# Value weights loaded as the second key stage opens, layer 0 four products later, the second attention step's exponentials among its products, one rotation put off

## The chip, the cores and the metric

The kernel runs on one core of a Trainium2 chip. A core has five engines with a queue of instructions each: TensorE (PE, matrix products into PSUM banks), VectorE (DVE), ScalarE (ACT), GpSimd (POOL) and SyncE (SP), which here only issues DMAs. ACT and POOL issue DMAs too. Each queue runs in its own order, and engines wait for one another by semaphores. The metric is the time of one execution on the device in microseconds.

## The reference

Two sequences of 512 rows of 1024 (`x`) and two contexts of 1024 rows of 1024 (`ctx`) run through four blocks, each added to `x`:

```python
x = x + fake_quant(layernorm(x)) @ fake_quant(ctx)                 # layer 0, part 1
x = x + layernorm(x) @ W.T + b + lora(layernorm(x)) * routing      # layer 0, part 2
q = rope(layernorm(x) @ wq)      # 32 heads of 128
k = rope(ctx @ wk)               # 8 key heads, each used by 4 query heads
v = ctx @ wv                     # 8 value heads
x = x + (softmax(q @ k.T / sqrt(128) + mask) @ v) @ wo
x = x + layernorm(x) @ W_up.T + lora of the top expert
```

Keys and values depend on the context only, so they can be computed before layer 0 has ended.

## The kernel before

**Products.** The large products of keys, values, queries, both linear maps and the output projection are done with seven products in place of eight (Strassen-Winograd). Sums of quarters of each operand are made first, on DVE (`left_steps`, `right_steps`), and `seven` or `seven_onto` then runs one generator per block of the output: each `yield` is one product, which the trace shows as 8 matmuls of 128x512 for keys and queries (4 in the code, an f32 one has two records) and 16 of 128x256 for values, into one of four PSUM banks of the tag "b". The results are put together by adds on DVE and a copy on ACT (lines 284 to 300), which also give the banks back. The other four PSUM banks are two double banks of the tag "wide", used for transposes and for attention's scores.

**Order of work.** PE's order is written out by hand: it is the order in which the program emits its instructions. The other engines are ordered by a scheduler, in two stretches excepted: the first key stages, and attention, where DVE and ACT (in attention POOL as well) run in emission order too.

**Stages.** Per sequence `b` there are two key stages and two value stages (`keys`, `keys`, `values`, `values`; `i` from 0 to 3), each with 14 products. `pair` interleaves the first two products of the two blocks of a stage. `weave(main, side, every)` runs a stage and calls `next(side)` after every second product. `side` is `layer_0()`: the quantized product of both sequences (`quantized_product`), cut by yields into small steps: loads of two context rows and their quantization on DVE (lines 194 to 198), layernorms of `x` (lines 163 to 176), transposes on PE (`turned`, line 423) with a copy and a row sum on ACT, then the products (line 460). The weights of a stage are loaded and summed by `quad_weights` after the stage before has been emitted: four DMAs of 512 KB on SP's queue (line 362) and four passes of DVE (lines 245 to 253, `quad_sums`). SP's queue also holds the writes of the keys to DRAM (line 486), the loads of context rows for layer 0 (line 413), and the writes of values.

**Rotations.** Keys and queries are rotated (`rope_steps`, lines 213 to 223): two copies on ACT swap the halves (216, 217), a pass of DVE multiplies by the cosine (219), and a multiply and an add on an engine of choice (222, 223) finish it. Queries are made for eight groups `q` of four heads (`queries`). For `q` below 7 all of a rotation is emitted at once on DVE. For `q` = 7 the products run inside attention, the second half of each rotation is put into a list `later`, and its multiply and add go to POOL; attention empties the list in the third phase of each step (`rotate`).

**Attention.** 64 heads run as a pipeline over steps `n` from -2. In step `n`, head `n+2` gets its scores (4 pairs of matmuls, line 759, and the add of the mask on DVE, 773), its maximum (`tree`, 781 to 787, then transposes 723 and a reduction 725), which travels to a row in DRAM and back to all partitions (`to_row`, line 732; `from_row`, line 738). Head `n+1` subtracts it (`place_maximum` copies it into a "b" bank, 801; `exponential`, 805 on DVE, 808 on ACT, sums on POOL 811 to 816). Head `n` multiplies by the values (822), turns its sum of exponentials into a reciprocal, sends it to a row (`turn_sum`) and reads it back (`old.den = from_row(old.den)`), and is normalized on POOL in the next step (833). Both reads and both row writes are on ACT's queue. A step has three phases, ended by yields: scores; tree, projection products (or, in the first steps, `extra` products of the last queries); and the third phase shown at lines 923 to 944.

The lines that the change touches in the stages are these:

```python
 weave(main, side, 2)
 if i < 3:
     w = quad_weights((wk, wv)[(i + 1) // 2], (i + 1) % 2)
```

and `extra = {-2: 3, -1: 3, 0: 2, 1: 2, 2: 2, 3: 1, 4: 1}`, the number of query products that each attention step takes in its second phase.

Of the kernel before, what the change touches and what calls it, by code (L numbers as in the profile page):

```python
# [21 lines left out]
NH, NKV, DH = 32, 8, 128  # L22
# [17 lines left out]
def decoder_kernel(  # L40
# [25 lines left out]
    nc = tc.nc  # L66
# [268 lines left out]
    def weave(main, side, every, skip=0):  # L335

        for i, _ in enumerate(main):
            if i >= skip and (i - skip) % every == 0:
                next(side, None)
# [15 lines left out]

    def quad_weights(dram, q):

        raw = []
        for mh in range(2):
            for ch in range(2):  # L360
                w = u4([P, 4, 256])
                nc.sync.dma_start(w, dram[q, mh, ch])
                raw.append(w)
        return quad_sums(raw)

    def quad_sums(raw):
        return left_sums(nc.vector, *raw, lambda: u4([P, 4, 256]))
# [288 lines left out]
        yield  # L656


    def queries(q, h_ops, w, later=None):

        def head(m):
            def product(i, acc, start):
                accumulate(
                    acc,
                    [(w[i - 1][:, c, ts(m, P)], h_ops[i - 1][:, c, :]) for c in range(4)],
                    start,
                )

            def finish(i, j, src):
                dst = u2([P, HALF]) if (i, j) == (0, 0) else src  # L670
                eng = nc.vector if later is None else nc.gpsimd
                yield from rope_steps(dst, src, 0, ATT_SCALE, eng)
                nc.sync.dma_start(q_d[j][4 * q + 2 * i + m], dst)

            def emit(i, j, src):
                steps = finish(i, j, src)
                next(steps)
                if later is None:
                    next(steps, None)
                else:  # L680
                    later.append(steps)

            return seven(product, emit)

        return head(0), head(1)
# [49 lines left out]
    def from_row(row):  # L735

        t = u2([P, S])
        nc.scalar.dma_start(t, row.partition_broadcast(P))
        return t
# [107 lines left out]
    def attention(extra):  # L847

        total = B * NH
        heads, outs, kv = {}, {}, {}
        stretches = iter(())

        def rotate():
            for rotation in extra["later"]:
                next(rotation, None)
            extra["later"].clear()

        def begin(n):
            if n >= total:
                return
            gg = n // GRP
            if gg not in kv:
                b, g = gg // NKV, gg % NKV
                kT = u4([P, S2])
                nc.sync.dma_start(kT, kT_d[b][g])
                v = u4([P, NKT, DH])
                nc.sync.dma_start(v, v_d[b][g // 2][:, :, ts(g % 2, DH)])  # L870
                kv[gg] = kT, v
                outs[gg] = u8([P, GRP, S])
            heads[n] = Head(n, kv[gg], outs[gg][:, n % GRP, :])

        begin(0)
        for n in range(-2, total + GRP + 1):
            new, mid, old = heads.get(n + 2), heads.get(n + 1), heads.get(n)
            begin(n + 3)
            if new:
                for j in range(4):  # L880
                    new.scores(j)
            yield

            if n - 1 in heads:
                heads.pop(n - 1).normalize()
            if n == GRP - 1 or n == NH:
                fetch_rows(n // NH)

            if GRP <= n <= total and n % GRP == 0:
                oT = outs.pop(n // GRP - 1)  # L890
                sums = u8([P, 3, 2, 256])
                places = iter(range(3))
                o_ops = left_sums(
                    nc.gpsimd,
                    oT[:, 0:2, 0:256],
                    oT[:, 2:4, 0:256],
                    oT[:, 0:2, 256:S],
                    oT[:, 2:4, 256:S],
                    lambda: sums[:, next(places)],
                )  # L900
                following = n // GRP - 1, o_ops
            tree = new.tree() if new else iter(())
            k = (n - 1) % GRP
            if n > GRP and k == 0:
                gg, o_ops = following
                stretches = projection(gg // NKV, o_ops, dict(w_ops))
            for _ in range(3 + k % 2 if n > GRP else 0):
                next(stretches, None)
                next(tree, None)
            if n > GRP and gg + 1 < B * NKV:  # L910
                for i in {2: (1, 6, 2), 3: (7, 5, 4, 3)}.get(k, ()):
                    w_ops[i] = output_operand((gg + 1) % NKV, i)
            for _ in range(extra.pop(n, 0)):
                for _ in range(2):
                    next(tree, None)
                next(extra["products"])
            if n == GRP:
                w_ops = {i: output_operand(0, i) for i in (1, 6, 2, 7, 5, 4, 3)}
            for _ in tree:
                pass  # L920
            yield

            if mid:
                mid.place_maximum()
            if old:
                old.turn_sum()
            elif new:
                new.turn_maximum()
            rotate()
            if old:  # L930
                old.attend(0)
            if mid:
                mid.exponential(0)
            if old:
                old.den = from_row(old.den)
                if new:
                    new.turn_maximum()
            if mid:
                mid.exponential(1)
            if new:  # L940
                new.nmx = from_row(new.nmx)
            if old:
                old.attend(1)
            yield
# [85 lines left out]
    w = [wk_raw[q][0:2] + [None] * 5 for q in range(2)]  # L1030
# [33 lines left out]
    side = layer_0()  # L1064
    for b in range(B):
        if b == 1:
            for ch in range(2):
                ctx_raw[2 * ch + 1] = context_quarter(1, ch, 1, nc.scalar)
            w = quad_weights(wk, 0)
            ctx_ops = context_sums(ctx_raw)  # L1070
        for i, stage in enumerate((keys, keys, values, values)):
            if (b, i) == (0, 0):
                continue
            if (b, i) == (0, 3):
                ctx_raw = [None] * 4
                for ch in range(2):
                    ctx_raw[2 * ch] = context_quarter(1, ch, 0, nc.scalar)
            if (b, i) == (0, 1):
                main = chain(*first[1])
            else:  # L1080
                main = pair(*stage(b, i % 2, ctx_ops, w))
            weave(main, side, 2)
            if i < 3:
                w = quad_weights((wk, wv)[(i + 1) // 2], (i + 1) % 2)
            if i == 1 and b == 1:
                for _ in side:
                    pass
                ab_t = u8([P, 2, D])
                a_t, b_t = ab_t[:, 0].rearrange("p (c m) -> p c m", c=NC), ab_t[:, 1]
                nc.sync.dma_start(a_t, a0T.rearrange("(c p) m -> p c m", p=P))  # L1090
                nc.gpsimd.dma_start(b_t, b0.partition_broadcast(P))
                tT = [None] * B
                fetch_rows(0)
                hs, steps = normed(0, u8, 2)
                side = chain(steps, routed(0, hs, a_t, b_t, tT))
# [18 lines left out]
    for b in range(B):  # L1114
        main = linear(b, token_sums(hs, eights()), w_ops, lambda: tT[b], bl_t)
# [10 lines left out]
    w = [quad_weights(wq, 0), quad_weights(wq, 1)]  # L1126
    side = query_norm(1)
    h_ops = [hb[0][0], hb[0][1]] + [None] * 5
    early = [head for q in range(2) for head in queries(q, h_ops, w[q])]
    for _ in range(2):  # L1130
        for head in early:
            next(head)
# [4 lines left out]
    )  # L1137
    later = []
    for q in range(NH // 4):
        heads = (  # L1140
            early[2 * q : 2 * q + 2]
            if q < 2
            else queries(q, h_ops, w, later if q == NH // 4 - 1 else None)
        )
        main = chain(*heads) if q < 2 else pair(*heads)
        for g in ((0,), (1,), (2,), (3,), (4,), (5,), (6, 7), ())[q]:
            output_sums(g)
        if q < NH // 4 - 1:
            for _ in main:
                pass  # L1150
            if q > 0:
                w = quad_weights(wq, q + 1)

    extra = {-2: 3, -1: 3, 0: 2, 1: 2, 2: 2, 3: 1, 4: 1}
    steps = attention({**extra, "products": main, "later": later})
    stats = all_moments(0)
    last = {"zT": [None] * B, "w": [None] * 7, "h": [None] * 7}
# [186 lines left out]
```

## Time and profile before

| | us |
|---|---|
| median of three runs | 2475.18 (2473.69 to 2479.97) |
| profiled execution | 2474.92 |
| its span | 2473.1 |
| PE busy in it | 2432.6 (98%) |
| DVE busy | 1835.2 (74%) |
| POOL busy | 1028.8 (42%) |
| ACT busy | 528.1 (21%) |
| granted clock of PE, mean | 0.993 |

The profile is of one execution. Its times start at the span's beginning. The stages of the first sequence's keys and values lie between 0 and some 225 us (the first value stage begins at 109), those of the second follow, the queries end at about 928 where attention begins, attention's last step ends near 2300, and the last linear map fills the rest. A busy share counts the time in which an engine works on an instruction; an idle stretch of PE stands in brackets ahead of the row that ended it, with the instruction whose end released it. Idle time of another engine costs nothing by itself; it matters only where PE waits for it.

### The profile page before, as it was taken

The page shows a single profiled execution, that of the slowest core. Times are in us where ns is not written, and L with a number is a line of the kernel's source. Part 1 is how long each engine was busy: PE and PEld are TensorE (multiplying, and loading weights), DVE is VectorE, ACT ScalarE, POOL GpSimd, SP SyncE. Part 2 cuts the span into 40 slices and gives each one's busy share as a digit, 9 for nine tenths or more (in the row PEclk, how much of TensorE's full clock was granted, in tenths as well). Part 3 has the DMA queues.
Part 4 walks back from the last instruction along what each step waited for, and adds up shares of the span by engine and source line. Part 5 has one row for each costly group of instructions (what it writes and reads, how often), then busy time and mean ns, then how long its engine had stood idle before and what let it go on. Part 6 is the DMA issues. An engine that isn't in the chain of part 4 may idle for free.

```text
span 2473.1 us, 19694 instructions
## 1 busy us (share of the span) xinstructions
PE 2432.6 (98%) x6856; PEld 1218.4 (49%) x6856; DVE 1835.2 (74%) x2020; ACT 528.1 (21%) x615; POOL 1028.8 (42%) x552
## 2 busy tenths in 40 slices
PE   8999999999999999999999999999999999999998
PEld 3477458654444444444444444444444444445453
DVE  4949674346886547898888888888888888886552
ACT  1211221001122222222222222222222222222100
POOL 0000010111000002686767767776767676767421
PEclk9999999999999999999999999999999999999999
DMA  5437142013895221344323432443334333323301
GB/s 181 179 120 255 69 146 97 22 68 111 296 333 187 74 98 41 106 128 115 103 76 90 115 95 81 128 149 89 105 110 129 79 94 108 112 72 103 128 26 43
DMA packets 148819, 288.02 MB, mean 116 GB/s; under 512 B 29360, under 2 KB 47296, under 8 KB 146416
## 3 DMA queue, kind: packets, MB, share of 16 engines
q1 hardware_dynamic: 107888, 244.35, 29.4%
q10 hardware_dynamic: 40400, 41.70, 6.9%
q8 instruction: 55, 0.90, 0.2%
q0 software_dynamic: 432, 0.71, 0.1%
q14 instruction: 44, 0.36, 0.1%
HBM read 223.54 MB, written 63.18 MB: 116 GB/s over the span
## 4 chain that ended last, share of the span: by engine, by line
PE 79%; DVE 8%; POOL 3%; issue 2%; DMA 2%; ACT 1%; SPq 0%; ACTq 0%; POOLq 0%; DVEq 0%
PE b L347 45%; PE wide L759 15%; PE b L822 14%; DVE u L805 2%; PE wide L723 2%; PE wide L460 1%; PE wide L204 1%; POOL u L815 1%; POOL u L814 1%; DVE u L783 1%; DMA u<-in_wo_dram 1%; DVE u L785 1%; PE wide L954 1%; DVE small L725 1%; DMA row<-small 1%
## 5 line engine op out<-in xcount | busy, mean ns | idle before, releaser
L347 PE MATMUL b<-u,u 128*128 128x512 f32 (+1 forms) x3648 | 1407.8, 544 | 19.1 <-DMA u<-in_ctxT_in_dram 7.8
L347 PEld LDWEIGHTS b<-u,u 128*128 128x128 f32 x3648 | 693.6, 191 | 698.7 <-issue 619.2
L822 PE MATMUL b<-u,u 128*128 128x512 f32 x1024 | 462.3, 595 | 0.0
L759 PE MATMUL wide<-u,u 128*128 128x512 f32 x1024 | 454.3, 595 | 7.2 <-DVE u L773 6.3
L773 DVE TENSOR_TENSOR u<-wide,u 128x1024 f32<-128x1024 f32 x256 | 312.9, 1224 | 133.1 <-PE wide L759 132.9
L808 ACT ACTIVATE u<-u 128x2048 f32<-128x2048 f32 x128 | 244.6, 1911 | 653.8 <-DVE u L805 619.9
L759 PEld LDWEIGHTS wide<-u,u 128*128 128x128 f32 x1024 | 193.9, 190 | 256.0 <-issue 176.7
L805 DVE TENSOR_TENSOR u<-u,b 128x2048 f32<-128x2048 f32 x128 | 290.2, 2268 | 0.0
L811 POOL TENSOR_TENSOR u<-u 128x1024 f32<-128x1024 f32 x64 | 151.4, 2366 | 319.8 <-ACT u L808 319.8
L822 PEld LDWEIGHTS b<-u,u 128*128 128x128 f32 x1024 | 187.3, 193 | 185.6 <-issue 185.6
L322 POOL TENSOR_TENSOR u<-u,u 128x512 f32<-128x512 f32 x120 | 188.7, 1592 | 197.5 <-DVE u L320 177.9
L320 DVE TENSOR_TENSOR u<-u,b 128x512 f32<-128x512 f32 x200 | 135.9, 680 | 135.4 <-PE b L347 135.4
L222 POOL TENSOR_TENSOR u<-u,sin_t 128x512 f32<-128x512 f32 x8 | 11.6, 1455 | 387.8 <-ACT u L217 387.8
L814 POOL TENSOR_TENSOR u<-u,u 128x1024 f32<-128x1024 f32 x64 | 150.8, 2356 | 35.6 <-ACT u L808 35.2
L815 POOL TENSOR_TENSOR u<-u,u 128x1024 f32<-128x1024 f32 x64 | 151.6, 2369 | 5.0
L833 POOL TENSOR_TENSOR u<-u,u 128x512 f32<-128x512 f32 x64 | 117.7, 1839 | 21.8 <-DMA u<-row 21.8
L216 ACT ACTIVATE u<-u 64x512 f32<-64x512 f32 x72 | 45.2, 628 | 356.1 <-DVE u L293 177.9
L603 POOL TENSOR_TENSOR u<-u,u 128x1024 f32<-128x1024 f32 x8 | 20.2, 2532 | 231.5 <-DVE u L168 228.9
L723 PEld LDWEIGHTS wide<-ident,u 128*128 128x128 f32 x512 | 80.1, 204 | 64.5 <-issue 54.3
L781 DVE TENSOR_TENSOR u<-u 128x1024 f32<-128x1024 f32 x64 | 110.4, 1725 | 0.0
L783 DVE TENSOR_TENSOR u<-u,u 128x1024 f32<-128x1024 f32 x64 | 106.1, 1658 | 0.2
L816 POOL TENSOR_TENSOR u<-u 128x512 f32<-128x512 f32 x64 | 101.4, 1584 | 5.0
(127 smaller groups left out, 1624.8 us busy)
## 6 DMA issues: line engine op xcount, KB each, us to landing
u<-row ACTq DMA_DIRECT2D x128, 256.0 KB, 3.7
u<-wo SPq DMA_DIRECT2D x64, 512.0 KB, 4.2
u<-in_wo_dram SPq DMA_DIRECT2D x48, 512.0 KB, 4.5
u<-in_wq_dram SPq DMA_DIRECT2D x32, 512.0 KB, 4.2
q<-u SPq DMA_DIRECT2D x64, 256.0 KB, 2.6
u<-in_wo_dram SPq DMA_DIRECT2D x16, 1024.0 KB, 8.1
wo<-u SPq DMA_DIRECT2D x32, 512.0 KB, 4.4
u<-q SPq DMA_DIRECT2D x64, 256.0 KB, 4.2
```

What stands on the lines that cost most here:

```text
L320: nc.vector.tensor_tensor(c, c, acc, ALU.add)
L322: nc.gpsimd.tensor_tensor(c, c, u, ALU.add)
L347: nc.tensor.matmul(acc, lhsT, rhs, start=start and k == 0, stop=k == len(pairs) - 1, skip_group_check=True,)
L759: nc.tensor.matmul(sc[:, ts(n, HALF)], self.kT[:, ts(2 * j + n, P)], self.qT, start=True, stop=True,)
L773: nc.vector.tensor_tensor(self.e[j // 2][:, js, :], sc.rearrange("p (k q) -> p k q", k=2), mask[j], ALU.add)
L783: nc.vector.tensor_tensor(m, m, e[1][:, 0:2, :], ALU.max)
L805: nc.vector.tensor_tensor(e, e, self.nmf.unsqueeze(1).to_broadcast([P, 4, S]), ALU.add)
L808: nc.scalar.activation(e, e, AF.Exp)
L811: nc.gpsimd.tensor_tensor(d, e[:, 0:2, :], e[:, 2:4, :], ALU.add)
L814: nc.gpsimd.tensor_tensor(d, d, e[:, 0:2, :], ALU.add)
L815: nc.gpsimd.tensor_tensor(d, d, e[:, 2:4, :], ALU.add)
L822: nc.tensor.matmul(self.acc, self.v[:, k, :], self.e[j][:, k % 4, :], start=(k == 0), stop=(k == NKT - 1),)
```

## The change

1. `quad_weights` is split into the loads (`raw_weights`) and the sums (`quad_sums`). In the second key stage of the first sequence the loads of the value weights are issued before the stage's products are emitted, and the sums after them. In the same stage layer 0 takes its first step four products later (`skip` = 4), so all its steps of both sequences come four products later.
2. `queries` takes the engine of the rotation as an argument, and the groups 6 and 7 both use the list `later`. For group 6, whose multiply and add stay on DVE, the list is emptied right after each product while the product's index is below 13; the rotation of the last product, the fourteenth, stays in the list until attention's first third phase.
3. `extra` gives the step -2 two and the step -1 four products in place of three and three. In step -1, the first with a head to exponentiate and none to finish, the copy of the maximum and the first exponential follow the second of the four products, and the second exponential the third, in place of the third phase.
4. In every later step the read of the denominators' row is emitted after the second exponential in place of after the first.

No instruction is added or taken away.

```diff
     def quad_weights(dram, q):
 
+        return quad_sums(raw_weights(dram, q))
+
+    def raw_weights(dram, q):
         raw = []
         for mh in range(2):
             for ch in range(2):
                 w = u4([P, 4, 256])
                 nc.sync.dma_start(w, dram[q, mh, ch])
                 raw.append(w)
-        return quad_sums(raw)
+        return raw
...
-    def queries(q, h_ops, w, later=None):
+    def queries(q, h_ops, w, eng, later=None):
...
-                eng = nc.vector if later is None else nc.gpsimd
...
-            for _ in range(extra.pop(n, 0)):
+            for i in range(extra.pop(n, 0)):
                 for _ in range(2):
                     next(tree, None)
                 next(extra["products"])
+
+                if mid and not old and i == 1:
+                    mid.place_maximum()
+                    mid.exponential(0)
+                if mid and not old and i == 2:
+                    mid.exponential(1)
...
-            if mid:
+            if mid and old:
                 mid.place_maximum()
...
                 old.attend(0)
-            if mid:
-                mid.exponential(0)
-            if old:
-                old.den = from_row(old.den)
+                if mid:
+                    mid.exponential(0)
                 if new:
                     new.turn_maximum()
-            if mid:
-                mid.exponential(1)
+                if mid:
+                    mid.exponential(1)
+                old.den = from_row(old.den)
...
             if (b, i) == (0, 1):
                 main = chain(*first[1])
+
+                raw = raw_weights(wv, 0)
+                weave(main, side, 2, 4)
+                w = quad_sums(raw)
             else:
                 main = pair(*stage(b, i % 2, ctx_ops, w))
-            weave(main, side, 2)
-            if i < 3:
-                w = quad_weights((wk, wv)[(i + 1) // 2], (i + 1) % 2)
+                weave(main, side, 2)
+                if i < 3:
+                    w = quad_weights((wk, wv)[(i + 1) // 2], (i + 1) % 2)
...
-    early = [head for q in range(2) for head in queries(q, h_ops, w[q])]
+    early = [head for q in range(2) for head in queries(q, h_ops, w[q], nc.vector)]
...
-        heads = (
-            early[2 * q : 2 * q + 2]
-            if q < 2
-            else queries(q, h_ops, w, later if q == NH // 4 - 1 else None)
-        )
+        heads = early[2 * q : 2 * q + 2]
+        if q > 1:
+            last_two = q >= NH // 4 - 2
+            heads = queries(
+                q, h_ops, w, (nc.vector, nc.gpsimd)[q == NH // 4 - 1], later if last_two else None
+            )
...
-            for _ in main:
-                pass
+            for i, _ in enumerate(main):
+
+                if i < 13:
+                    for rotation in later:
+                        next(rotation, None)
+                    later.clear()
...
-    extra = {-2: 3, -1: 3, 0: 2, 1: 2, 2: 2, 3: 1, 4: 1}
+    extra = {-2: 2, -1: 4, 0: 2, 1: 2, 2: 2, 3: 1, 4: 1}
```

## The prediction

> **What bounds the kernel now.** I read the page's busy rows first: TensorE (PE) 2432.6 us of a span of 2473.1, DVE 1835.2, POOL 1028.8, ACT 528.1. Only 40.5 us of the span have no matmul, so the change can bring a few us at most, and only where it fills one of these holes. Which they are is told by the view of waits, for PE alone (line that waited, who released it: total us, times, longest):
>
> ```profile
> PE b L347 <- DMA u<-in_ctxT_in_dram: 7.8, 3, 4.0
> PE wide L759 <- DVE u L773: 6.3, 5, 3.6
> PE b L347 <- DMA u<-in_wv_dram: 4.0, 1, 4.0
> PE wide L723 <- POOL u L816: 2.9, 3, 1.7
> PE b L347 <- DVE u L291: 2.4, 2, 1.5
> PE b L347 <- ACT u L284: 1.6, 1, 1.6
> ```
>
> Row 1 is the start of the program, which the change leaves alone. Rows 2, 3 and 6 lie where the change works; rows 4 and 5 it touches. The timeline of PE places them (start, length, line, [idle before, releaser]):
>
> ```profile
> 113.42 12.31 PE L347 MATMUL b<-u,u 128*128 128x256 f32 x48 [4.04 <-DMA u<-in_wv_dram]
> 127.77 7.17 PE L347 MATMUL b<-u,u 128*128 128x256 f32 x32 [1.59 <-ACT u L284]
> ...
> 928.41 3.67 PE L759 MATMUL wide<-u,u 128*128 128x512 f32 x8 [0.44 <-PE b L347]
> 933.66 3.70 PE L759 MATMUL wide<-u,u 128*128 128x512 f32 x8 [1.58 <-DVE u L773]
> ...
> 972.81 5.40 PE L759 MATMUL wide<-u,u 128*128 128x512 f32 x8 [3.60 <-DVE u L773]
> ```
>
> One product of keys, values or queries takes 3.44 us of PE wherever nothing holds it (24 matmuls of 128x512 in 10.46 us less their overlap of 0.14, for three). The rows at 113.42 and 972.81 also run slow: 48 matmuls, three products, in 12.31 instead of 10.3 us, and 8 score matmuls in 5.40 instead of 3.67. The stretch 950 to 1000 has a granted clock of 0.97, the others beside it 1.00.
>
> **The clock, rule and row.** The row: holes of 4.04 and 3.60 us are followed by 2.0 and 1.73 us of slow matmuls; holes of 1.59, 1.58 and 1.53 (at 343.11) by none. The Trainium skill, "TensorE: Matmul & The Clock Gate", section "Why this matters for your kernels", says to leave no gap over about 3 us, since a window of idle halves the clock. Thus the two large holes cost 6.0 and 5.3 us. The rule also speaks against this change: a new hole of 3.7 us, which I find below, would cost 5.4 us by the rule and 3.7 if it falls just short, as nothing between 1.6 and 3.6 is shown. I take half the surcharge.
>
> **Part 1: value weights and layer 0 (109 to 350 us).** From 109.38 to 150.04 PE does nine products (31.0 us) and four turns of layer 0 (1.77): 40.66 less 32.8 is 7.9 us lost. The hole of 4.04 is SP's queue: the four value loads stand behind four key writes, the first of which waits for its rotation:
>
> ```profile
> 91.30 18.24 SPq L486 DMA_DIRECT2D kT<-u  x4
> 109.59 0.42 SPq L362 DMA_DIRECT2D u<-in_wv_dram  x1
> ```
>
> Issued at the stage's opening they pass these writes and land some 20 us early, so 4.04 and the slow clock's 2.0 go. The 1.59 is ACT's order: L284 stood behind the copy of a turn that waited 5.48 us for PE; with layer 0 four products later three L284/L508 copies come ahead of it. Recovered: 7.8.
>
> What is late next. (a) In key stage 2 the moments of layer 0 and the last two context loads come later; the loads now stand behind the value loads (4 x 512 KB, 1.4 us of issue after the first) and key writes. DVE's L291, at 101.19 now, falls to about 103.5 where PE wants its bank at 102.5: -1.0 (0 to -2). (b) The whole of layer 0 sits four products later, so its batch 1 steps now meet the opening of batch 1's first key stage. DVE's backlog there, from the end of the last value product (225) to the first keys' L291, is 18.3 us of operand sums (four L245 to L253, of 1.2, and four L259 to L267, of 2.3, of which some are done before), two quantizations and two rotations: about 24 us by their rows. L291 starts at 256.07 now, 2.3 us ahead of PE's need at 258.41. With the turns gone from between the products PE's need comes at about 249.5 counted in the old clock, and L291 at 251.3 to 253.9: -1.8 to -4.4, by 1.7 more if the clock drops. I take -2.2, the near end, because DVE is 47.33 of 50 us busy in that stretch and what layer 0 no longer asks of it comes off its queue. (c) The 1.53 before 343 (L291 behind a DVE pass that POOL's L603 slows) may go or grow: 0 (+-1.5). The weave's other steps stay beside full products. Sum: 7.8 - 1.0 - 2.2 = **+4.6** (0 to +7.8).
>
> **Part 2: the first attention steps (925 to 985).** Lost there now: 0.44 + 1.58 + 3.60 + 1.73 = 7.35. The first two are two rotations (L219 to L223, 2 us each on DVE) in front of the first score sum L773. The last rotation is put off into the step's third phase, so L773 comes two us sooner: +1.6, +0.3 of the 0.44. It goes to DVE's order there, ahead of the next scores' L773: -0.5.
>
> The 3.60 is DVE's order: at 967.14 two exponential subtractions L805 (4.47 us) stand ahead of the L773 that would free the "wide" bank. The change issues them among four products of the step instead of three, and two instead of three in the step before; the sum of products stays. PE has then 13.8 us of products over L805, so this hole and its 1.73 go: +5.3.
>
> It adds a wait. There are four "b" banks. The maximum's copy L801 takes one, and gives it back only after the second L805. In the new order of allocation the fourth product of the step gets that very bank. What stands before on each engine:
>
> ```profile
> 958.47 0.59 ACT L216 ACTIVATE u<-b 64x512 f32<-64x512 f32 x1 [9.52 <-PE b L347]
> 959.08 0.59 ACT L217 ACTIVATE u<-b 64x512 f32<-64x512 f32 x1
> 959.57 0.58 ACT L801 COPY b<-u 128x512 f32<-128x512 f32 x1
> ...
> 967.14 4.47 DVE L805 TENSOR_TENSOR u<-u,b 128x2048 f32<-128x2048 f32 x2
> ```
>
> L801 is behind a rotation's L216 and L217, which wait for their own product. In the change's time that product ends near 956.9, L801 near 958.6, the first L805 at 961, L288 and the second L805 at 964.1; PE could begin the fourth product at 960.4. A hole of 3.7 us, from 1 (if L801 gets ahead) to 3.8, with half of the surcharge 0.85: -4.5. Behind it on PE stands the rest of the step; on DVE nothing is held. Sum: 1.9 - 0.5 + 5.3 - 4.5 = **+2.2** (0 to +6.5).
>
> POOL's sums of the first head (L811 to L816, 8.3 us) begin some 8 us earlier. The Trainium skill, "GPSIMD Engine Reference", section "1. Specifications", has POOL share its SBUF interface with DVE instructions of two SBUF inputs. The row: the tree's L781 beside L816 took 1.71 us at 979.38, against 1.22 alone. Moved ahead, the sums leave the tree of the third step alone; by rule and row together 0.5 us of DVE, off the path: 0.
>
> **Part 3: the steady steps (985 to 2300).** In every later step the read of the denominators' row (from_row, on ACT's queue) moves behind the second exponential. Where the row's write is slow, the read now blocks ACT:
>
> ```profile
> 1637.70 0.35 ACTq L738 DMA_DIRECT2D u<-row  x1
> 1638.08 0.44 ACTq L732 DMA_DIRECT2D row<-small  x1
> ...
> 1638.57 1.91 ACT L808 ACTIVATE u<-u 128x2048 f32<-128x2048 f32 x1 [3.95 <-DMA row<-small]
> ```
>
> The second L808 is 3.95 us late, POOL's L814 to L816 after it, and PE then waits for L816 (0.49 and 0.39; the same at 1998, 1.73). With the read behind them these 2.6 us go. In return the row lands some 2.8 us later in all steps: exponential 1.91 and its gap of 0.88. Who waits is POOL's L833 and what is behind it:
>
> ```profile
> L833 POOL TENSOR_TENSOR u<-u,u 128x512 f32<-128x512 f32 x64 | 117.7, 1839 | 21.8 <-DMA u<-row 21.8
> 1446.94 0.33 ACTq L738 DMA_DIRECT2D u<-row  x1
> ...
> 1457.88 2.26 POOL L833 TENSOR_TENSOR u<-u,u 128x512 f32<-128x512 f32 x1
> ```
>
> From issue to use there are 10.9 us; a read lands 3.7 us after its issue (the page's median of 128), so 7.2 are free and 2.8 of them are used up: 0. The next maximum's read is queued behind it, but its own row is written later. Sum: **+2.6** (-2 to +3).
>
> **The sum.** 4.6 + 2.2 + 2.6 = 9.4. The profiled execution took 2474.92 us (span 2473.1, 1.8 around it), 0.26 below the median shown of 2475.18. Forecast **2465.5 us**, -0.39%. About 0.3%, 7.4 us, is what a measurement of this kernel tells from no change: below 2467.8 is faster, above 2482.6 slower.
>
> **Rivals.**
> - *Nothing late takes the holes' place*: the bank comes free in time, and DVE keeps up. 7.8 + 6.7 + 2.6 = 17.1: 2458. For it: the free margins of 2 us come from rows, and an error of 2 removes each new wait. Against: L801's place in ACT's queue. Chance 0.22.
> - *The holes only move*: DVE's backlog at the first keys of batch 1 crosses the clock's threshold (-4.4 - 1.7), the bank's wait costs 5.4 in full, and the den reads give back one of 2.6: 0.7 + 1.3 + 1.6 = 3.6: 2471, within the bound. For it: DVE 47.33 of 50 us in 200 to 250. Chance 0.28.
> - *Slower, by the denominators' read*: L833 waits on POOL in every fourth step, where the four operand sums L245 to L253 of the projection follow it, and pushes L811 to L816 late. It decides once a row lands over 10.9 us after the old issue: the slow writes above used up 7. If in each of 16 such steps 1.0 us reaches PE, -16, with Parts 1 and 2 +6.8: 2484. Against: L833 waits for its row 21.8 us in all now, and little of that reaches PE. Chance 0.10.
> - *The change does not do what it says*: the issue order of the changed program has the value loads ahead of the context's and one rotation put off, so this has no chance of note.
>
> **The numbers.** Forecast 0.40 (2461 to 2470), rivals 0.22, 0.28, 0.10. Three quarters of the forecast's own range lies below 2467.8, so faster is 0.30 + 0.22 + 0.04 of the second rival = 0.56; slower 0.08; same 0.36. The range goes from 2455, past the best rival, to 2477; it leaves out the slow rival and the far ends.
>
> **What would show it.** Right: no hole before L347 near 109 and a first value stage of granted clock 1.00; a hole of about 3.7 us in the second attention step whose releaser is L805, none of 3.6 at the third's scores; no ACT L808 of some 3.9 us wait; a hole released by L291 near 250. Wrong: row waits of L833 well over 22 us with L816 behind them, or layer 0's end pushed into the second key stage of batch 1.

## The result and the profile after

The changed kernel takes **2479.39 us** (median of 21 runs, 2476.43 to 2486.55) against 2475.18 of the kernel before (21 runs, 2472.67 to 2480.23). The ratio is 1.0017, 95% interval 1.0011 to 1.0024: slower by 4.2 us, clear of the noise of so many runs and within the 0.3% bound named in the prediction. The forecast was 2465.5 with a range up to 2477. The profiled execution took 2479.7 (span 2477.0). Lines after some 360 stand 2 to 7 lines further down than before: L803 is the old L801, L807 the old L805, L606 the old L603.

The view of waits, PE alone (who waited, for whom: total us, times, longest):

```profile
PE b L347 <- DVE u L291: 6.1, 4, 3.7
PE b L347 <- ACT u L284: 5.2, 1, 5.2
...
PE wide L761 <- DVE u L775: 1.6, 4, 0.6
```

The 4.0 on the value weights and the 1.6 on L284 are gone, the 6.3 on the mask add is 1.6. In their place stand 6.1 on L291, a new 5.2 on L284, and four small waits of 1.0 to 1.5 us. PE's timeline says where (start, length, [idle before, releaser]):

```profile
90.53 14.00 PE L347 MATMUL b<-u,u 128*128 128x512 f32 x32 [0.38 <-DVE u L293]
106.22 31.61 PE L347 MATMUL b<-u,u 128*128 128x512 f32 x128 [1.68 <-DVE u L291]
251.32 3.70 PE L347 MATMUL b<-u,u 128*128 128x512 f32 x8 [1.16 <-DVE u L219]
256.50 0.62 PE L426 MATMUL wide<-ident_b,u 128*128 128x128 bf16 x8 [1.48 <-DVE u L198]
260.82 9.39 PE L347 MATMUL b<-u,u 128*128 128x512 f32 x16 [3.70 <-DVE u L291]
293.33 3.70 PE L347 MATMUL b<-u,u 128*128 128x512 f32 x8 [1.04 <-DMA u<-in_wk_dram]
...
367.55 5.52 PE L347 MATMUL b<-u,u 128*128 128x256 f32 x16 [5.17 <-ACT u L284]
...
973.05 3.70 PE L347 MATMUL b<-u,u 128*128 128x512 f32 x8 [1.25 <-DVE u L288]
```

The first value stage runs without a hole, attention's entry has lost its big one, and the loss sits between 250 and 370 us, in the second sequence's keys and values, of which the change's own lines say nothing. Behind the two large holes the matmuls run slow: the 16 matmuls of two key products take 9.39 us where 7.08 is usual, the 16 of one value product 5.52 instead of some 3.6. The granted clock was 0.91 between 240 and 280.

Cut into stretches at the same instruction of each trace, from PE's timeline, the time went so (us):

| stretch | before | after | gain |
|---|---|---|---|
| first loads, to PE's seventh product matmul | 12.7 | 14.3 | -1.6 |
| from there to the second sequence's first key product | 220.2 | 215.1 | +5.1 |
| its key stages | 117.2 | 125.9 | **-8.8** |
| its value stages | 108.9 | 116.1 | **-7.2** |
| layer 0's linear map and the queries | 469.4 | 468.1 | +1.4 |
| attention's first three scores (entry) | 49.8 | 44.7 | +5.1 |
| steady steps, to the first transpose of the last map's gates (L988, now L995) | 1320.6 | 1318.5 | +2.1 |

The first row differs in the same code from one execution to the next (11.9 to 14.5 us over the traces of this study), and so does the fifth (467.8 to 472.1).

### The profile page after: what moved, and what is told of

Same layout as the page of the kernel before. It is cut to its first block, busy times and chain, and to the rows that moved or that the text cites. A ratio compares the mean times of both kernels' runs of the same rounds, so it can differ in the third digit from the quotient of the medians.

```text
span 2477.0 us, 19654 instructions
## 1 busy us (share of the span) xinstructions
PE 2435.3 (98%) x6848; PEld 1216.2 (49%) x6856; DVE 1841.4 (74%) x2020; ACT 524.1 (21%) x615; POOL 1031.2 (42%) x552
## 4 chain that ended last, share of the span: by engine, by line
PE 53%; DVE 5%; issue 1%; POOL 1%; ACT 0%; POOLq 0%; DVEq 0%; ACTq 0%
PE b L347 19%; PE wide L761 16%; PE b L824 15%; PE wide L725 2%; DVE u L807 1%; PE wide L961 1%; DVE u L787 1%; DVE u L785 0%; DVE u L320 0%; DVE small L727 0%; POOL u L816 0%; POOL u L817 0%; DVE u L775 0%; ACT u L810 0%; PE wide L204 0%
## 5 line engine op out<-in xcount | busy, mean ns | idle before, releaser
L775 DVE TENSOR_TENSOR u<-wide,u 128x1024 f32<-128x1024 f32 x256 | 313.0, 1224 | 125.0 <-PE wide L761 124.8
L807 DVE TENSOR_TENSOR u<-u,b 128x2048 f32<-128x2048 f32 x128 | 290.3, 2269 | 3.0 <-ACT b L803 3.0
L816 POOL TENSOR_TENSOR u<-u,u 128x1024 f32<-128x1024 f32 x64 | 150.7, 2354 | 30.8 <-ACT u L810 30.5
L835 POOL TENSOR_TENSOR u<-u,u 128x512 f32<-128x512 f32 x64 | 115.8, 1810 | 23.5 <-DMA u<-row 23.5
L606 POOL TENSOR_TENSOR u<-u,u 128x1024 f32<-128x1024 f32 x8 | 20.2, 2533 | 247.4 <-DVE u L168 247.4
L216 ACT ACTIVATE u<-u 64x512 f32<-64x512 f32 x72 | 45.2, 628 | 360.0 <-DVE u L293 173.6
L727 DVE TENSOR_REDUCE small<-wide 128x4 f32<-128x512 f32 x128 | 87.2, 682 | 15.2 <-PE wide L725 15.2
```

Of the source, the lines that this page charges most:

```text
L775: nc.vector.tensor_tensor(self.e[j // 2][:, js, :], sc.rearrange("p (k q) -> p k q", k=2), mask[j], ALU.add)
L807: nc.vector.tensor_tensor(e, e, self.nmf.unsqueeze(1).to_broadcast([P, 4, S]), ALU.add)
L816: nc.gpsimd.tensor_tensor(d, d, e[:, 0:2, :], ALU.add)
```

## The experiments

Each ratio is against the kernel before on the same chip (medians of 2475.3 to 2475.6); "attention alone" means the change without its part 1. The theory was A: the shift of layer 0 by four products makes the two new places of loss. Its rival B: the early loads make them, by pushing other loads back on SP's queue.

**The change without the shift.**

```diff
-                weave(main, side, 2, 4)
+                weave(main, side, 2)
```

> The change with layer 0 left at its old place (value weights still issued as the second key stage opens). Theory A, the shift of layer 0 by four products makes the new holes at batch 1's keys (1.16, 1.48, 3.70 with the clock, 1.04) and before its first value stage (5.17 with the clock): all of them go, the hole of 4.04 on the value weights stays away; about 2463 us. Theory B, the early loads make them, because the context and x loads behind them on SP's queue come late: the holes stay, 2477 to 2480.

2474.66 us, ratio 0.9992 (0.9983 to 1.0001). Both theories missed. The second sequence's keys took 117.1 and its values 108.9 us, as before, so both places of loss are the shift's doing. But the stretch ahead of them took 226.1 us, 6 more than before. DVE's timeline of this kernel, in the second key stage:

```profile
90.89 0.81 DVE L194 TENSOR_SCALAR u<-u,qp_inv_x,qp_x_zp 128x1024 f32<-128x1024 f32 x1 [1.99 <-DMA u<-in_ctx_in_dram]
91.62 0.68 DVE L293 TENSOR_TENSOR u<-u,b 128x512 f32<-128x512 f32 x1
```

The quantization L194 stands ahead of L293, which gives a bank back, and waits for context rows whose load is now behind the value weights: PE lost 3.26 us there, 1.02 and 0.75 after it, and 4.12 in the value stage, there for L284. So the early loads alone do take the wait on the value weights away, and cost 6 us more than they bring; the shift removes most of that cost and brings its own later.

**Part 1 alone, and attention alone.** The kernel before with part 1; and the change without part 1.

```diff
-                raw = raw_weights(wv, 0)
-                weave(main, side, 2, 4)
-                w = quad_sums(raw)
+                weave(main, side, 2)
+                w = quad_weights(wv, 0)
```

(the diff of attention alone)

> Before with part 1 of the change alone (early loads and the shift), attention as before. If the parts add up as the two traces say, attention's gain of 7.2 us is missing: 2479.4 + 7.2 = about 2486.5 us, attention's first scores begin some 10 us later than in the kernel before. If the parts need one another: 2480 or less.

> The change without part 1: stages as before, attention as in the change. If the parts add up: 2475.2 - 5.1 (entry) - 2.1 (steady steps) = about 2468 us, with holes of 0.50, 0.41 and 1.25 at attention's entry and none of 3.6. If attention's gain came from a shifted start only: about 2475.

Part 1 alone: 2486.39 us, 1.0040 (1.0025 to 1.0055). Attention alone: 2468.91, 0.9969 (0.9956 to 0.9982). Both as expected to 0.9 us (though with part 1 alone attention's first scores began 14.1 us later than before, not some 10): the parts add up, and part 1 costs 11 us by itself.

**The shift without early loads.**

```diff
-                raw = raw_weights(wv, 0)
-                weave(main, side, 2, 4)
-                w = quad_sums(raw)
+                weave(main, side, 2, 4)
+                w = quad_weights(wv, 0)
```

> The change with layer 0 four products later, but the value weights loaded at their old place. Theory A (the shift makes the holes at batch 1's keys and before its first value stage): both stay, about 13 us with the clock, and the hole of 4.0 on the value weights is back: 2482 to 2486. Theory B (these two need the early loads as well): 2472 or less.

2476.53 us, 1.0005 (0.9996 to 1.0013). The two holes stayed, keys 127.6 and values 116.2 us, so the early loads have no part in them. The hole of 4.0 did not come back, which theory A had wrong, and the 1.68 at 106 was gone too. SP's queue shows why:

```profile
83.50 3.69 SPq L365 DMA_DIRECT2D u<-in_wv_dram  x4
91.78 7.78 SPq L489 DMA_DIRECT2D kT<-u  x3
```

With layer 0 later, the scheduler itself puts the four value loads ahead of the key writes that they had waited behind. The explicit early loading adds nothing to the shift; it only moves context loads back.

**The shift made up for.** Two steps of layer 0 are taken at the opening of the second value stage, where DVE has room.

```diff
                 main = pair(*stage(b, i % 2, ctx_ops, w))
+                if (b, i) == (0, 3):
+                    next(side)
+                    next(side)
                 weave(main, side, 2)
```

> The change, with the two layer-0 steps that the shift puts off made up for as the second value stage of batch 0 opens, so that layer 0 of batch 1 stands against the products as in the kernel before. Theory A: the 1.16, 1.48 and 3.70 at batch 1's first keys with their slow clock, and the 5.17 with its own, all go: 2479.4 less some 15, about 2464. Theory B (DVE's backlog there comes of something else): holes of over 3 us stay at 250 to 262, 2472 or more.

2462.80 us, 0.9945 (0.9928 to 0.9961), as theory A said. Keys 117.2 and values 108.9 us. The view of windows, from 240 to 280 us, of the change and of this kernel (length, then busy us and instructions of PE, weight loads, DVE, ACT, POOL, then granted clock, DMA share, GB/s):

```profile
240.00:280.00 40.00, 33.66 (x93) 14.90 (x92) 38.23 (x58) 12.45 (x21) 0.00 (x0) 0.91 0.26 90
```

```profile
240.00:280.00 40.00, 40.00 (x136) 18.59 (x134) 28.75 (x51) 12.15 (x21) 0.00 (x0) 1.00 0.09 34
```

With layer 0 late, DVE is busy 38.23 of 40 us and PE 33.66 at a granted clock of 0.91; in step, DVE has 28.75 and PE is full. What makes DVE late can be read from three timelines, of ACT's and SP's queues and of DVE. The kernel before has:

```profile
205.72 2.08 ACTq L399 DMA_DIRECT2D u<-in_ctxT_in_dram  x2
...
228.32 1.23 DVE L245 TENSOR_TENSOR u<-u,u 128x1024 f32<-128x1024 f32 x1
...
256.07 0.67 DVE L291 TENSOR_TENSOR u<-u,b 128x512 f32<-128x512 f32 x1
```

and the changed kernel:

```profile
215.86 4.81 ACTq L402 DMA_DIRECT2D u<-in_ctxT_in_dram  x2
...
224.40 0.33 SPq L513 DMA_DIRECT2D v<-u  x1
224.77 0.43 SPq L365 DMA_DIRECT2D u<-in_wk_dram  x1
...
232.78 1.22 DVE L245 TENSOR_TENSOR u<-u,u 128x1024 f32<-128x1024 f32 x1 [5.87 <-DMA u<-in_wk_dram]
...
260.07 0.69 DVE L291 TENSOR_TENSOR u<-u,b 128x512 f32<-128x512 f32 x1
```

PE begins the second sequence's first key product at 232.92 in the kernel before and at 229.40 in the changed one. Counted from there, the two loads of the next context were issued 27.2 and 25.5 us ahead before, and only 13.5 and 9.1 us ahead after; the last of the four loads of key weights 12.5 us ahead before, and 4.6 after, behind a write of values on SP's queue. DVE has L245, which needs these weights, in front of the other operand sums, and stood idle for 5.87 us. So 13.4 us of operand sums fell between the first key product and L291, where 5.6 had. Layer 0's norms and quantizations in that stretch did not grow: 9.1 us against 12.6. L291 gave PE its bank at 260.76, when PE had stood ready since 257.1; the holes of 1.16 and 1.48 come of the same lateness (the second is a turn of layer 0 in PE's own order, whose input L198 has only just written).

The other three kernels with layer 0 late show the same, an idle stretch of 6.2 to 6.4 us ahead of that L245, and none of the ten with layer 0 in step does. In two of the three, PE waited for an operand sum itself (L262: 1.18 us in the shift without early loads, 0.48 with the bias add on DVE). That the shift makes the loads late, and the catch-up cures it, is shown; what holds them back is not. The context loads moved by 13.7 us, and four products take 13.8 (an estimate, four times 3.44), so buffers that layer 0 still holds are likely. No run moved the loads alone.

**The second hole, tested alone.** The changed kernel with layer 0's bias add on DVE.

```diff
-            nc.gpsimd.tensor_tensor(rows(b, t), rows(b, t), b_t, ALU.add)
+            nc.vector.tensor_tensor(rows(b, t), rows(b, t), b_t, ALU.add)
```

> The change with layer 0's bias add (L606, 8 passes of POOL) given to DVE. Theory A, the hole of 5.17 before batch 1's first value stage comes of DVE passes with two SBUF inputs that run at 2.83 instead of 0.68 us beside these POOL passes, delay L300 and with it the rotation's copies that stand ahead of L284 on ACT: the hole goes with its slow clock, 7 us, 2472. Theory B, DVE is simply behind there, whatever POOL does: the hole stays or grows by the 4 passes of 1.2 us moved to DVE, 2479 to 2485.

2470.79 us, 0.9984 (0.9975 to 0.9992): as theory A on POOL's passes said, 8.6 us less than the changed kernel. The values stage takes 108.9 us again; the 3.70 at the keys stays (keys 126.7 us), so the two holes are separate. In the changed kernel the timelines of DVE, POOL and ACT have:

```profile
350.79 2.52 DVE L168 TENSOR_SCALAR u<-u,small,small 128x1024 f32<-128x1024 f32 x1
353.96 2.83 DVE L219 SCALAR_TENSOR_TENSOR u<-u,u 128x512 f32<-128x512 f32 x1
356.72 2.84 DVE L222 TENSOR_TENSOR u<-u,u 128x512 f32<-128x512 f32 x1
...
362.16 2.83 DVE L222 TENSOR_TENSOR u<-u,sin_t 128x512 f32<-128x512 f32 x1
350.42 2.34 POOL L606 TENSOR_TENSOR u<-u,u 128x1024 f32<-128x1024 f32 x1 [123.45 <-DVE u L168]
353.40 5.60 POOL L606 TENSOR_TENSOR u<-u,u 128x1024 f32<-128x1024 f32 x2 [0.63 <-DVE u L168]
361.56 2.88 POOL L606 TENSOR_TENSOR u<-u,u 128x1024 f32<-128x1024 f32 x1 [2.56 <-DVE u L168]
...
365.62 0.63 ACT L216 ACTIVATE u<-u 64x512 f32<-64x512 f32 x1 [4.10 <-DVE u L300]
366.26 0.63 ACT L217 ACTIVATE u<-u 64x512 f32<-64x512 f32 x1
366.91 1.07 ACT L284 COPY u<-b 128x512 f32<-128x512 f32 x2
```

A DVE pass that reads two tiles of SBUF beside a POOL pass takes up to 2.84 us in place of 0.68. It waits for its turn: each held pass ends 0.55 us after the POOL pass beside it (L222 at 359.56 after POOL's 359.00, the last one at 364.99 after 364.44). A pass that reads one operand from PSUM is not held; the kernel before shows one in the middle of a POOL pass:

```profile
342.38 0.67 DVE L291 TENSOR_TENSOR u<-u,b 128x512 f32<-128x512 f32 x1
341.87 2.80 POOL L603 TENSOR_TENSOR u<-u,u 128x1024 f32<-128x1024 f32 x1 [2.60 <-PE b L347]
```

The kernel before also has three rotation passes held (2.83 us at 331.54, 2.84 at 336.97, 2.28 at 345.24), all ahead of its first value product at 350.08. In the changed kernel that product starts at 355.31, and the held passes lie around it. They delay L300 and with it the last rotation of the key stage, whose copies L216 and L217 stand on ACT ahead of L284, and L284 holds PE's bank until 367.5. With the adds on DVE the same L219 and L222 take 0.69.

**Attention's entry, taken apart.** On attention alone: the rotation not put off; and the exponentials in the third phase with products 3 and 3.

```diff
-                if i < 13:
+                if True:
```

```diff
-                if mid and not old and i == 1:
-                    mid.place_maximum()
-                    mid.exponential(0)
-                if mid and not old and i == 2:
-                    mid.exponential(1)
...
-            if mid and old:
+            if mid:
                 mid.place_maximum()
...
                 old.den = from_row(old.den)
+            elif mid:
+                mid.exponential(0)
+                mid.exponential(1)
...
-    extra = {-2: 2, -1: 4, 0: 2, 1: 2, 2: 2, 3: 1, 4: 1}
+    extra = {-2: 3, -1: 3, 0: 2, 1: 2, 2: 2, 3: 1, 4: 1}
```

> Part 1 undone, and the last rotation of the seventh group of queries not put off. If the rotation in front of the first L775 makes the 1.58 at attention's entry: it comes back, 1.0 to 1.6 us above 2468.9. If not: no change, and no hole released by L775 there.

> Part 1 undone, and the exponentials of the second step (n = -1) back in its third phase, with products 3 and 3. If the two subtractions in front of L775 make the 3.60 and its slow clock: it comes back whole (5.3 us) and the 1.25 goes: 4 us above 2468.9, 2473. If the gain at attention's entry is the rotation's: no change.

The rotation back: 2468.63 us, 0.9975 (0.9966 to 0.9984), no different in time from attention alone; the hole of 1.56 on L775 is back in the trace, and the entry takes 45.85 us against 44.65. The exponentials back: 2473.93, 0.9995 (0.9987 to 1.0003), and the entry takes 50.29. So the exponentials among the products bring 5.6 us and the rotation 1.2, which the time can't resolve; put off without them, it makes the entry no shorter than before (49.80), as a hole of 2.08 opens at a later score.

**The moved read.** Attention alone, with the denominators' read at its old place.

```diff
+                old.den = from_row(old.den)
                 if new:
                     new.turn_maximum()
                 if mid:
                     mid.exponential(1)
-                old.den = from_row(old.den)
```

> Part 1 undone, and the read of the denominators' row back at its old place, so of the change only attention's entry is left. If the moved read is worth what the traces say, this is 2 us slower than the same without this (2468.9): 2471, with PE waits on POOL's last sum (0.5 to 1.7) in steps where a row is slow, and ACT exponentials some 3.9 us late. If it is worth nothing: 2469.

2470.23 us, 0.9977 (0.9967 to 0.9988), against 2468.91 and 0.9969: the intervals overlap. In the traces with the read at its old place (three of them) ACT stands idle for over 2 us ahead of three of the 64 second exponentials (3.37, 2.51 and 2.75 here); in all with the read moved, never for more than 0.95. So ACT is freed as forecast, but the steady steps took 1317.7 us in both of these two traces, with one PE wait of 0.41 for it: what the move is worth in time, 1.3 us by the medians, is not clear of the noise.

**Loads on POOL's queue.** Attention alone, the value loads at their old place but issued by POOL.

```diff
-    def raw_weights(dram, q):
+    def raw_weights(dram, q, queue=nc.sync):
...
-                nc.sync.dma_start(w, dram[q, mh, ch])
+                queue.dma_start(w, dram[q, mh, ch])
...
-                w = quad_weights(wv, 0)
+                w = quad_sums(raw_weights(wv, 0, nc.gpsimd))
```

> Part 1 undone (attention as in the change), with the first value weights loaded at their old place in the program but on POOL's DMA queue, which has nothing else to do there. If the hole of 4.0 on these weights is only their place behind four key writes on SP's queue, it goes with its slow clock (6 us less than 2468.9) and no hole at the second key stage comes in its place, as the context loads keep theirs: 2463. If the buffers come free late or this queue's loads are slow, the hole stays: 2469 or more.

2465.83 us, 0.9956 (0.9942 to 0.9971), against 2468.91 and 0.9969: half of the 6 us expected, and the intervals overlap. The hole on the weights went and no hole came at the keys, but PE then stood 3.45 us at 119 for L284, which ACT reaches only after the norms' and rotations' instructions. L284 ran at 118.60, and at 119.12 in the kernel before, where PE had come 4 us later and did not meet it: the 4.0 had been hiding this wait.

**The two fastest versions.** The shift without early loads with the catch-up's two steps added; and the same with the bias add on DVE, by the diffs above.

> The change with the value weights loaded at their old place in the program, and the two put-off steps of layer 0 made up for at the second value stage. If the shift alone already lets these loads past the queue (the shift-only run had no hole at 109), and the early loads only push the context loads back (holes of 0.70 and 1.65 at 89 and 105 in the catch-up run): these two go, 2460. If the early loads are needed: the hole of 4.0 is back, 2467.

> The shift with the catch-up, loads at their old place (e9), and layer 0's bias add on DVE in place of POOL. If the 1.5 before 340 (L291 after a rotation's multiply slowed by the bias add on POOL) is the shared access too: it goes, 1.5 us below e9, about 2458.5. If DVE is simply behind there: as e9 or slower.

2460.97 us, 0.9944 (0.9931 to 0.9956), and 2458.02, 0.9934 (0.9922 to 0.9947). The holes ahead of 89 and 105, which the catch-up still had from the early loads (0.70 and 1.65 us), are gone in both, and in the second the keys take 115.4 us instead of 117.1: the old hole of 1.5 us near 340 was POOL's and DVE's turns as well. The second is 17 us faster than before; between the two the intervals overlap.

## Why the prediction was wrong

- **Part 1, what it recovers** (7.8): right. The holes of 4.04 and 1.59 and the slow clock went (7.2 us, the 5.1 of the table and the 2.1 of (a)). The credit, given to the early loads, was half wrong: the shift alone closes both holes, and the early loads alone put a wait of 4.12 on L284 in place of the one on the weights.
- **(a), the second key stage** (-1.0): holes of 0.38 and 1.68, -2.1, just past its range; caused by the early loads, as its reason said.
- **(b), the first keys of batch 1** (-2.2): **the step that failed**, with (c). It measured -8.8. The place, the engine and the instruction were right. What failed is that DVE was taken to work off "about 24 us by their rows" from the end of the last value product on, without a wait for its operands. From PE's first key product (229.40) to L291 (260.07) there were 30.7 us, 27.3 of work and 3.4 of the idle stretch of 5.87 on the key weights. The prediction looked for late loads in (a) and put those of the next keys at nothing. PE would have needed the bank at 254.5 but for this stage's own first holes, and got it 6.3 us later, where 1.8 to 4.4 was forecast and the near end taken, "because DVE is 47.33 of 50 us busy in that stretch and what layer 0 no longer asks of it comes off its queue". That did come off (9.1 us for 12.6), but 7.8 more of operand sums took its place. The slow clock, left out of the price, cost 2.3 and a late load of the second key weights 1.04: 9.7 in all, where before had lost 1.5 in these stages. Two figures of this term were also off: four passes of 1.2 and four of 2.3 make 14.0 us and not 18.3, and the first sequence's values end at 232.9 in the kernel before and not at some 225.
- **(c), the hole before 343** (0, +-1.5): failed too, -7.2. The prediction named POOL's add as the cause of the old hole, but gave its next meeting 0 without working it out. Four products of shift put the same held passes on the last rotation of the key stage, in front of ACT's L284: a hole of 5.17 us and 1.9 of slow clock.
- **Part 2** (+2.2): +5.1. The mechanisms were right, one size was off: the fourth product waited 1.25 us, for L288 behind the first subtraction, and not 3.7 with a share of the clock for the second. By its releaser it was another bank than the one the prediction gave it.
- **Part 3** (+2.6): ACT's late exponentials went as forecast; +2.1 in the pair of traces, of which the experiment, 1.3 us with intervals that overlap, settles nothing.
- **The rivals.** The nearest was "the holes only move", right in kind: DVE's backlog at batch 1's keys, and PE slow behind it. Its 2471 is 8.4 us short of the measured time; the meeting with POOL's add alone cost 7.2. L833's read (L835 now) waited 23.5 us in all against 21.8, so the slower rival did not come.

Of the sum of 9.4, parts 2 and 3 gave 7.2 where 4.8 was forecast, and part 1 gave -10.9 where +4.6 was. The rest of the 3.9 us between the two spans is the first loads and the linear stretch, which differ between executions.

## What to carry to other kernels

When a side job is shifted against a main stream, every later meeting of the two moves, not only the one that the shift is for: list all places where the side job's instructions stand ahead of one that frees a buffer, and where loads of the main stream are issued behind the side job, through to the end of it, and price each with the new alignment. A backlog counted by its rows is a lower bound: ask also when its inputs arrive. If the shift helps one place, give it back in the next stretch where the engine has room: here two steps taken early turned +4 us into -13. Rows that run slow in the old trace (2.83 for 0.68) tell of a neighbour; ask whether the change makes them meet more often.

## What was not expected of the hardware

DVE's passes with two SBUF operands did not run beside POOL's add of 128x1024: they waited for its end, and it for theirs. Where L219 (361.55) began 0.01 us ahead of POOL's pass, it kept its 0.69 and POOL took 2.88 in place of 2.34. The Trainium skill, "GPSIMD Engine Reference", section "1. Specifications", names this contention and DVE instructions with two SBUF inputs among those that suffer it, and these rows agree; that the loss is what is left of the other's pass, and 2.83 against 0.68 us at worst, is what the traces add. Why L168, which reads one tile and two columns, was held too is not shown. In attention the same turn-taking accounts for the smaller loss (1.71 against 1.22): L781 began at 979.38, when POOL's L816 had 0.63 us left, and ended 1.09 after it.

The cost of PE's slow phase does not follow the length of the hole: 1.9 us after 4.04 (12.31 less the 10.46 of three products), 1.7 after 3.60, 2.3 after 3.70 and 1.9 after 5.17, but 1.6 after another hole of 3.70, in part 1 alone (8.68 us in place of 7.08).
